# Moving the head of two attentions into the stages before them, in one kernel of four macaron layers

## The chip, the cores and the metric

The kernel runs on one core of a Trainium2 chip. A core has five engines, each with its own instruction queue: TensorE (PE, matmuls; PEld is its weight load), VectorE (DVE), ScalarE (ACT), GpSimd (POOL) and SyncE (SP, DMA issue). An engine takes its queue in order; waits between engines are semaphores. The metric is the device time of one execution in microseconds, as the median of several executions. One more execution is profiled, and all rows of profiles and traces come from it.

## The reference, cut to what matters

The input is eight sequences of 512 tokens of width 128. It runs through a chain of residual blocks, each fed with a layer norm of the running x:

```python
x = x + 0.5 * L0_ffn(ln(x)); x = x + L0_attn(ln(x)); x = x + 0.5 * L0_ffn(ln(x))
x = x + 0.5 * L1_ffn(ln(x)); x = x + L1_attn(ln(x)); x = x + 0.5 * L1_ffn(ln(x))
x = x + 0.5 * L2_ffn(ln(x)); x = x + L2_attn(ln(x)); x = x + 0.5 * L2_ffn(ln(x))
x = x + 0.5 * L3_ffn(ln(x)); x = x + L3_attn(ln(x)); x = x + 0.5 * L3_ffn(ln(x))
```

The change touches these parts:

- `L1_ffn`: sixteen experts of width 64, of which each token takes four (chosen by group and rank), and one shared expert of width 128; `silu(x Wg) * (x Wu)`, weighted, times `Wd`.
- `L1_attn`: sixteen heads of width 8 over the sequence, softmax, with positional encoding before and a norm after. `L3_attn`: the same shape, causal, without encoding and norm.
- `L2_ffn`: a gated feed-forward net whose inputs are rounded in blocks of 16 to a grid of eight values. `L2_attn`: a gated linear recurrence along the tokens. `L3_ffn`: relu net of width 512.

## The kernel before, in words

Everything stays on the chip between the load of x and the store. Tokens lie on partitions in x (`x[b]` is 128 x 4 x 128 for sequence b); the stages transpose to features on partitions. `_STAGES` at the end lists the order: `l0_ffn`, `l0_attn`, `l0_ffn`, `l1_ffn`, `l1_attn`, `experts_layer2`, `l3_attn`, `l3_ffn`. Each stage opens its own pools of SBUF and PSUM and closes them at its end. A scheduler orders the instructions of each engine when the program is built, by dependences, free buffers and the order of emission; `in_order` (L373) ties chosen engines to the order of emission.

**The experts** (`l1_ffn` L836, `experts` L901, `routed` L869). For every sequence there are ten steps. Step e does two matmuls with the weights of two experts (tiles "pg" and "pu"), Silu on ACT (L920), the product with pu on DVE (L921), the product with the token's shares of these experts (tile "big", two PSUM banks, L928), and the down projection of the step before into "po". The last step turns the result back (yT, tile "mm", L938 to L940) and adds it to x (L433). Between the steps `routed(b + 1)` makes the next sequence's norm, transposes and choice of experts; its `ranks` use DVE, and POOL at L957. In PSUM it holds eight banks: po 1, mm 1, pg 2, pu 2, big 2.

**The second use of the experts** is woven with all of layer 2 and the first relu net in `experts_layer2` (L1111): `rounded_ffn` twice, `recurrence` and `relu_ffn` hand in pieces with a slot each, and the list of all pieces, sorted by slot, is emitted in that order. `_EXPERTS`, `_STARTS`, `_STEPS` and the tables `_ROUNDED_FFN`, `_RECURRENCE`, `_RELU_FFN` hold the slots; a slot is a place in the order and no time. There "mm" and "pg" have two buffers, "pu" one.

**The attention** (`attention` L1448). For a sequence, `projections` gives seven pieces: four of the norm (L405 to L413), the transpose xT (L1574), q and k (two matmuls, then "lead", L1541, and "trail", L1543, which together carry the full precision in two rounded halves) and the values v (L1559). `spread_out` (four times, g = 0 to 3) puts four heads at a time onto blocks of 32 partitions (qkT, L1587). `maxima` computes scores once only to take each row's maximum: a matmul of 32 rows into the tile "first" (three buffers), in the causal case a mask added by a second matmul, then a reduction on DVE (L1620). There are 64 such matmul pieces per sequence; the causal case packs short rows together, so that DVE has 44 reductions for them. After every 16 a copy on POOL spreads the maxima (L1626). `maxima_turned` transposes them (L1658 to L1662, tile mT). Then `weighted` computes the scores again, subtracts the maximum by a further matmul with mT, takes the exponential on ACT (L1728) and multiplies with v into "av". In the loop of `weighted(b)`, whose PE order is fixed, the maxima of sequence b + 1 are done two per step, and projections of sequence b + 2 and the end of sequence b - 1 come at the slots of `_SLOTS`.

At the start of each attention nothing of this is there yet for sequence 0:

```python
            for b in range(2):
                for piece in self.projections(b):
                    piece()
                for g in range(4 if b == 0 else 2 if causal else 1):
                    self.spread_out(b, g)
            for _ in range(64 + _SLOTS[key]["lead"]):
                read = next(maxima)()
                if read:
                    read()
            self.maxima_turned(0)
```

So the projections of sequences 0 and 1, the spreads, the 64 maxima of sequence 0 and four of sequence 1 (`lead`) stand ahead of the first weighted score.

Of the kernel before, what the change touches and what calls it, by code (L numbers as in the profile page):

```python
# [26 lines left out]
P = 128  # L27
# [175 lines left out]
def _attention_pack(p, wq, bq, wk, bk, wv, bv, wo, bo):  # L203
# [40 lines left out]
_IN_ORDER = 4.5  # L244
_STARTS = (18, 27, 46, 64)
_STEPS = (8, 8, 8, 6.5)
# [4 lines left out]
    "x_in": -5,  # L251
# [10 lines left out]
    "apply": 1.5,  # L262
    "turned": 2.5,
# [4 lines left out]
    "sums": 7.5,  # L268
    "added": 7.5,
}  # L270
_RELU_FFN = {
    "stats": -1,
    "apply": 0,
    "turned": 2.5,
    "wide": (3.5, 4, 5, 5),
    "product": 6,
    "added": 7.5,
}


class _Kernel:
    def __init__(self, ctx, tc, u, packs, out):
# [3 lines left out]
        const = ctx.enter_context(tc.tile_pool(name="const", bufs=1))  # L286
        self.ln_pool = ctx.enter_context(tc.tile_pool(name="ln", bufs=3))
# [13 lines left out]


# [134 lines left out]
    def l0_ffn(self):  # L437
        nc, tc = self.nc, self.tc
        w = lambda n: self.w["l0f", n]
        with ExitStack() as s:  # L440
            keep = s.enter_context(tc.tile_pool(name="keep", bufs=1))
            sb = s.enter_context(tc.tile_pool(name="sb", bufs=2))
            ps = s.enter_context(tc.tile_pool(name="ps", bufs=2, space=bass.MemoryType.PSUM))
# [36 lines left out]
    def l0_attn(self):  # L480
# [8 lines left out]
        with ExitStack() as s:  # L489
            keep = s.enter_context(tc.tile_pool(name="keep", bufs=1))  # L490
            sb = s.enter_context(tc.tile_pool(name="sb", bufs=2))
            ps = s.enter_context(tc.tile_pool(name="ps", bufs=3, space=bass.MemoryType.PSUM))
# [343 lines left out]
    def l1_ffn(self):  # L836
# [3 lines left out]
        with ExitStack() as s:  # L840
            self.ps = s.enter_context(tc.tile_pool(name="ps", bufs=2, space=bass.MemoryType.PSUM))
            self.rings = {"mm": 1, "pg": 2, "pu": 2}
# [3 lines left out]
            for b in range(NB):  # L846
                ahead = self.routed(b + 1) if b + 1 < NB else iter(())
                experts = self.experts(b)
                for step in range(10):
                    ordered = self.both if (b, step) in self.aside_at else ()  # L850
                    with self.in_order(*ordered):
                        next(experts)
                        next(ahead, None)
                        if (b, step) in self.aside_at:
                            next(self.aside_at[b, step], None)
                for _ in ahead:
                    pass

    def open_experts(self, s):
        nc, tc = self.nc, self.tc  # L860
        keep = s.enter_context(tc.tile_pool(name="keep", bufs=1))
        self.sb = s.enter_context(tc.tile_pool(name="sb", bufs=2))
# [194 lines left out]
    def layer2_constants(self, ctx):  # L1057

        nc = self.nc
        keep = ctx.enter_context(self.tc.tile_pool(name="layer2_keep", bufs=1))  # L1060
# [29 lines left out]
        for name in ("w_gate", "w_up"):  # L1090
# [5 lines left out]
            pt = self.ps.tile([P, NC, P], F32, name="mm", bufs=1)  # L1096
# [8 lines left out]
        pt = self.ps.tile([P, NC, P], F32, name="mm", bufs=1)  # L1105
# [5 lines left out]
    def experts_layer2(self):  # L1111

        tc = self.tc
        with ExitStack() as s:
            self.fsb = s.enter_context(tc.tile_pool(name="fsb", bufs=2))
            self.ps = s.enter_context(tc.tile_pool(name="ps", bufs=2, space=bass.MemoryType.PSUM))
# [11 lines left out]
            def switch():  # L1128
                inner.close()
                self.asb = s.enter_context(tc.tile_pool(name="asb", bufs=2))  # L1130
# [10 lines left out]
            todo.append((_EXPERTS * NB - .001, switch))  # L1141
            todo.sort(key=lambda t: t[0])
# [226 lines left out]
    def l3_ffn(self):  # L1369
# [4 lines left out]
        with ExitStack() as s:  # L1374
            sb = s.enter_context(tc.tile_pool(name="sb", bufs=2))
            ps = s.enter_context(tc.tile_pool(name="ps", bufs=2, space=bass.MemoryType.PSUM))
# [30 lines left out]
    def attention_constants(self, ctx):  # L1407
# [4 lines left out]
        keep = ctx.enter_context(self.tc.tile_pool(name="heads", bufs=1))  # L1412
# [35 lines left out]
    def attention(self, key, causal):  # L1448
# [9 lines left out]
        nc, tc = self.nc, self.tc  # L1458
        with ExitStack() as s:
            keep = s.enter_context(tc.tile_pool(name="keep", bufs=1))  # L1460
            sb = s.enter_context(tc.tile_pool(name="sb", bufs=2))
            ps = s.enter_context(tc.tile_pool(name="ps", bufs=2, space=bass.MemoryType.PSUM))
            self.key, self.causal, self.sb, self.ps = key, causal, sb, ps
            self.bv = keep.tile([P, L], F32, name="bv")
            nc.gpsimd.tensor_copy(
                self.bv.rearrange("p (c d) -> p c d", c=NC), self.wide(self.w[key, "bv"])
            )
            self.seqs = [{} for _ in range(NB)]
            maxima = (m for b in range(NB) for m in self.maxima(b))
            for b in range(2):  # L1470
                for piece in self.projections(b):
                    piece()
                for g in range(4 if b == 0 else 2 if causal else 1):
                    self.spread_out(b, g)
            for _ in range(64 + _SLOTS[key]["lead"]):
                read = next(maxima)()
# [3 lines left out]
            with self.in_order(mybir.EngineType.PE):  # L1480
                for b in range(NB):
                    between = self.between(b)
                    for at, step in enumerate(self.weighted(b)):
                        step([m for m in (next(maxima, None), next(maxima, None)) if m])
# [3 lines left out]
            for piece in self.attended(NB - 1):  # L1488
                piece()

# [21 lines left out]
    def pair(self):  # L1512
        return self.ps.tile([P, 2, L], F32, name="pair")

    def projections(self, b):

        nc, sb, key = self.nc, self.sb, self.key
        w = lambda n: self.w[key, n]
        q = self.seqs[b]
# [3 lines left out]
        def end():  # L1523
            xn = q["xp"]
            norm[3]()
            if key == "l1a":
                q["xp"] = sb.tile([P, NC, D], F32, name="xp", bufs=4)
# [3 lines left out]
        def turned():  # L1531
            q["xT"] = self.turned(q["xp"], "xT")

        def halves():
            p = self.pair()
            q["lead"] = sb.tile([P, 2, L], F32R, name="lead", bufs=1)
# [327 lines left out]
```

## Time and profile before

| what | value |
|---|---|
| median of 3 runs | 2401.47 us (2400.5 to 2409.54) |
| the profiled execution | 2393.91 us |
| its span in the trace | 2392.2 us |
| mean granted clock of PE | 0.928 |
| PE busy | 2111.3 us (88%) |
| DVE busy | 1639.6 us (69%) |
| ACT busy | 1268.1 us (53%) |
| POOL busy | 660.8 us (28%) |
| share of the chain that ended last | PE 56%, DVE 24%, POOL 8%, ACT 7% |

Busy times add up what an engine did over the whole span; matmuls are pipelined and their ends are modelled, so a busy PE is not PE at its peak. The granted clock is the share of full speed that TensorE got. The last instruction of `l1_ffn` that writes x starts at 747.12 us, that of `experts_layer2` at 1859.46 us, by the trace. The costliest group is the reduction of `maxima` (864 of them, 534.8 us on DVE), the second the exponential (512, 436.3 us on ACT); both attentions are in these groups.

### The profile page before, as it was taken

The page shows a single profiled execution, that of the slowest core. Times are in us where ns is not written, and L with a number is a line of the kernel's source. Part 1 is how long each engine was busy: PE and PEld are TensorE (multiplying, and loading weights), DVE is VectorE, ACT ScalarE, POOL GpSimd, SP SyncE. Part 2 cuts the span into 40 slices and gives each one's busy share as a digit, 9 for nine tenths or more (in the row PEclk, how much of TensorE's full clock was granted, in tenths as well). Part 3 has the DMA queues.
Part 4 walks back from the last instruction along what each step waited for, and adds up shares of the span by engine and source line. Part 5 has one row for each costly group of instructions (what it writes and reads, how often), then busy time and mean ns, then how long its engine had stood idle before and what let it go on. Part 6 is the DMA issues. An engine that isn't in the chain of part 4 may idle for free.

```text
span 2392.2 us, 30012 instructions
## 1 busy us (share of the span) xinstructions
PE 2111.3 (88%) x10907; PEld 1011.7 (42%) x10967; DVE 1639.6 (69%) x3830; ACT 1268.1 (53%) x1855; POOL 660.8 (28%) x923
## 2 busy tenths in 40 slices
PE   7679999879998988999987999897778999999989
PEld 3344444434444433333333444355544444444434
DVE  5566775478886888888817889889864556666611
ACT  3546664323332276777762447667674145555554
POOL 1123443023211011111112234456552023333330
PEclk9779998989998599999997999999999779999999
DMA  3000000000000000000000000000000000000001
GB/s 123 1 1 1 1 1 1 14 10 1 1 1 1 0 1 1 1 1 1 1 1 7 1 1 1 1 0 1 1 0 1 0 1 1 1 1 1 1 1 35
DMA packets 10036, 13.08 MB, mean 5 GB/s; under 512 B 416, under 2 KB 8736, under 8 KB 9760
## 3 DMA queue, kind: packets, MB, share of 16 engines
q1 hardware_dynamic: 7776, 10.11, 1.3%
q8 instruction: 86, 1.41, 0.2%
q10 hardware_dynamic: 2112, 1.05, 0.2%
q14 instruction: 62, 0.51, 0.1%
HBM read 9.06 MB, written 2.10 MB: 5 GB/s over the span
## 4 chain that ended last, share of the span: by engine, by line
PE 56%; DVE 24%; POOL 8%; ACT 7%; issue 4%; DMA 0%; ACTq 0%; DVEq 0%; SPq 0%; POOLq 0%
PE pair L314 11%; PE av L314 8%; PE first L314 7%; PE mm L314 7%; PE po L314 5%; DVE max L1620 3%; PE pu L314 3%; ACT e L1728 3%; PE pg L314 3%; PE ck L314 2%; DVE act L921 2%; PE pr L314 2%; POOL ge L957 1%; PE ph L314 1%; DVE act L928 1%
## 5 line engine op out<-in xcount | busy, mean ns | idle before, releaser
L1620 DVE TENSOR_REDUCE max<-first 128x1 f32<-128x512 f32 (+3 forms) x864 | 534.8, 664 | 193.4 <-PE first L314 169.8
L1728 ACT ACTIVATE e<-pair 128x1024 f32<-128x1024 f32 (+3 forms) x512 | 436.3, 864 | 240.6 <-PE pair L314 227.8
L314 PE MATMUL first<-qkT 32*128 32x512 f32 (+3 forms) x1024 | 337.2, 474 | 29.5 <-DVE max L1620 28.1
L314 PE MATMUL pair<-qkT 32*128 32x512 f32 (+3 forms) x1024 | 223.7, 456 | 20.9 <-ACT e L1728 14.6
L314 PE MATMUL av<-e,v 128*32 128x512 f32 (+3 forms) x2048 | 239.7, 537 | 1.0
L314 PEld LDWEIGHTS pair<-qkT 32*128 32x128 f32 x1024 | 95.7, 186 | 233.7 <-ACT e L1728 133.4
L314 PE MATMUL pair<-mT,max_rows 32*128 32x512 f32 (+3 forms) x1024 | 191.5, 375 | 1.8 <-DVE mT L1662 1.8
L314 PEld LDWEIGHTS first<-qkT 32*128 32x128 f32 x1024 | 152.5, 198 | 94.5 <-DVE max L1620 86.2
L920 ACT ACTIVATE act<-pg 128x512 f32<-128x512 f32 x144 | 85.6, 596 | 195.3 <-PE pg L314 130.8
L1730 POOL TENSOR_SCALAR_AFFINE_SELECT e<-e 128x256 f32<-128x256 f32 x256 | 103.4, 407 | 252.4 <-ACT e L1728 252.0
L314 PE MATMUL pu<-xT,w_moe 128*128 128x512 f32 x288 | 154.9, 621 | 11.6 <-DVE act L921 10.9
L314 PE MATMUL po<-act,w_moe 128*128 128x512 f32 x288 | 157.2, 631 | 6.9 <-DVE act L928 4.3
L314 PE MATMUL pg<-xT,w_moe 128*128 128x512 f32 x288 | 152.4, 616 | 2.9 <-ACT h L1213 1.6
L921 DVE TENSOR_TENSOR act<-act,pu 128x512 f32<-128x512 f32 x144 | 97.8, 679 | 32.3 <-PE pu L314 26.8
L1626 POOL COPY copies<-max 128x128 f32<-128x128 f32 x64 | 22.7, 410 | 343.8 <-DVE max L1620 343.8
L314 PEld LDWEIGHTS pair<-mT,max_rows 32*128 32x128 f32 x1024 | 97.2, 189 | 3.6 <-DVE mT L1662 3.3
L928 DVE TENSOR_TENSOR act<-act,big 128x512 f32<-128x512 f32 x128 | 86.4, 678 | 11.6 <-PE big L314 10.5
L1587 ACT CAST qkT<-pair 128x1024 fp32r<-128x1024 f32 x64 | 64.7, 1013 | 42.0 <-PE pair L314 41.5
L314 PEld LDWEIGHTS pu<-xT,w_moe 128*128 128x128 f32 x288 | 51.5, 195 | 75.5 <-issue 37.8
L314 PEld LDWEIGHTS po<-act,w_moe 128*128 128x128 f32 x288 | 48.8, 192 | 63.9 <-issue 26.1
L423 PE MATMUL mm<-w_const,xn 128*128 128x128 f32 x192 | 38.9, 320 | 40.9 <-DVE xn L340 25.0
L314 PEld LDWEIGHTS pg<-xT,w_moe 128*128 128x128 f32 x288 | 52.0, 195 | 54.1 <-issue 42.8
(402 smaller groups left out, 4230.5 us busy)
## 6 DMA issues: line engine op xcount, KB each, us to landing
w_moe<-in_moe SPq DMA_DIRECT2D x1, 2392.0 KB, 14.0
out<-x SPq DMA_DIRECT2D x8, 256.0 KB, 2.3
x<-in_u ACTq DMA_DIRECT2D x4, 256.0 KB, 6.5
x<-in_u SPq DMA_DIRECT2D x4, 256.0 KB, 6.5
w_mixer<-in_l0a SPq DMA_DIRECT2D x1, 960.5 KB, 8.2
w_mixer<-in_l1a SPq DMA_DIRECT2D x1, 769.0 KB, 4.1
w_ffn<-in_l0f SPq DMA_DIRECT2D x1, 578.0 KB, 7.3
w_ffn<-in_l2f SPq DMA_DIRECT2D x1, 560.0 KB, 3.3
```

Of the source, the lines that this page charges most:

```text
L314: self.nc.tensor.matmul(out, lhsT, rhs, start=start, stop=stop)
L423: self.nc.tensor.transpose(pt[:, c, :], xn[:, c, :], self.ident)
L920: nc.scalar.activation(act, pg, AF.Silu)
L921: nc.vector.tensor_tensor(act, act, pu, ALU.mult)
L928: nc.vector.tensor_tensor(act, act, pw[:, e % 2, :], ALU.mult)
L957: nc.gpsimd.tensor_tensor(ge.rearrange(flat), ge.rearrange(flat), self.wide(before, m), ALU.mult)
L1587: self.nc.scalar.copy(t, p)
L1620: nc.vector.tensor_reduce(mx[:, c, j, gs[0] : gs[-1] + 1], sc, AX.X, ALU.max, negate=True)
L1626: nc.gpsimd.tensor_copy(copies[:, :, :, :, g], mx[:, :, :, g].unsqueeze(3).to_broadcast([P, NC, 4, 8]),)
L1728: nc.scalar.activation(e[:, :, :n], sc[:, :, :n], AF.Exp, scale=scale)
L1730: nc.gpsimd.affine_select(e[:, :, :P], e[:, :, :P], pattern=[[0, 2], [1, P]], compare_op=ALU.is_ge, fill=0.0, base=0, channel_multiplier=-1,)
```

## The change

The head of an attention (the value bias bv, seven pieces of `projections(0)`, four of `spread_out(0, g)`, 64 of `maxima(0)`) becomes a generator of 75 pieces, `attention_head`, that begins before the stage in front of it has ended. In `l1_ffn` it begins at step 31 of 80 (b = 3, step 1) and goes on every 0.6 of a step; in `experts_layer2` it begins at slot 84 and goes on every 0.55 of a slot. While it runs there it borrows that stage's PSUM: "pair" becomes the experts' "big" (one buffer), "first" becomes "mm" (two buffers). For that, `l1_ffn` gives one bank of "pu" to "mm". The tiles that outlive the stage lie in a pool "early" on the other side of SBUF. All pools are made with `reuse_waits="tile"`. `seqs` becomes `turns` in the attention, since both stages now hold their own state at once. Slots of layer 2 change, and `_IN_ORDER` with them.

```diff
-_IN_ORDER = 4.5
-_STARTS = (18, 27, 46, 64)
-_STEPS = (8, 8, 8, 6.5)
+_IN_ORDER = 3
+_STARTS = (18, 27, 46, 68)
+_STEPS = (8, 8, 8, 6)
...
 _ROUNDED_FFN = {
-    "x_in": -5,
+    "x_in": -4,
...
 _RECURRENCE = {
-    "apply": 1.5,
-    "turned": 2.5,
+    "apply": 2.5,
+    "turned": 3,
...
-    "sums": 7.5,
-    "added": 7.5,
+    "sums": 8,
+    "added": 8,
...
 _RELU_FFN = {
-    "stats": -1,
-    "apply": 0,
-    "turned": 2.5,
-    "wide": (3.5, 4, 5, 5),
-    "product": 6,
-    "added": 7.5,
+    "stats": -2,
+    "apply": 2,
+    "turned": 4.5,
+    "wide": (5.5, 6, 7, 7),
+    "product": 8,
+    "added": 11.5,
...
+_HEADS = {"l1a": (31, 0.6), "l3a": (84, 0.55)}
+
+def _heads_at(key, step):
+    first, each = _HEADS[key]
+    return sum(step <= first + k * each < step + 1 for k in range(75))
...
+    def pool(self, name, bufs, **kw):
+        return self.tc.tile_pool(name=name, bufs=bufs, reuse_waits="tile", **kw)
...
     def l1_ffn(self):
-            self.rings = {"mm": 1, "pg": 2, "pu": 2}
+            self.rings = {"mm": 2, "pg": 2, "pu": 1}
...
                 for step in range(10):
+                    at = 10 * b + step
+                    if at == _HEADS["l1a"][0]:
+                        self.begin_attention("l1a", False)
+                    heads = _heads_at("l1a", at)
                     ordered = self.both if (b, step) in self.aside_at else ()
                     with self.in_order(*ordered):
...
+                    for _ in range(heads):
+                        next(self.head)
...
     def experts_layer2(self):
+            first, each = _HEADS["l3a"]
+            todo.append((first - .001, partial(self.begin_attention, "l3a", True)))
+            todo.extend((first + k * each, lambda: next(self.head)) for k in range(75))
             todo.sort(key=lambda t: t[0])
...
     def attention(self, key, causal):
         with ExitStack() as s:
+            s.push(self.begun.pop_all())
+            self.sb = s.enter_context(self.pool("sb", 2))
+            self.ps = s.enter_context(self.pool("ps", 2, space=bass.MemoryType.PSUM))
+            self.banks = {"pair": ("pair", 2), "first": ("first", 3)}
+            for _ in self.head:
+                pass
+            for piece in self.projections(1):
+                piece()
+            for g in range(2 if causal else 1):
+                self.spread_out(1, g)
+            for _ in range(_SLOTS[key]["lead"]):
+                read = next(self.all_maxima)()
...
+    def begin_attention(self, key, causal):
+        self.key, self.causal = key, causal
+        self.begun = ExitStack()
+        self.early = self.begun.enter_context(self.pool("early", 1, side="right"))
+        self.banks = {"pair": ("big", 1), "first": ("mm", 2)}
+        self.turns = [{} for _ in range(NB)]
+        self.all_maxima = (m for b in range(NB) for m in self.maxima(b))
+        self.head = self.attention_head()
+
+    def attention_head(self):
+        self.bv = self.early.tile([P, L], F32, name="bv")
+        self.nc.gpsimd.tensor_copy(
+            self.bv.rearrange("p (c d) -> p c d", c=NC), self.wide(self.w[self.key, "bv"])
+        )
+        for piece in self.projections(0):
+            piece()
+            yield
+        for g in range(4):
+            self.spread_out(0, g)
+            yield
+        for _ in range(64):
+            read = next(self.all_maxima)()
+            if read:
+                read()
+            yield
```

The tiles xp, xT, lead, trail, max, copies and qkT of even sequences move to "early"; their number of buffers per sequence stays the same.

## The prediction, made before the changed kernel was run

> **What bounds the kernel now.** I read the slices of the page first, to see which engine is full where.
>
> ```profile
> PE   7679999879998988999987999897778999999989
> ...
> DVE  5566775478886888888817889889864556666611
> ...
> PEclk9779998989998599999997999999999779999999
> ```
>
> PE is nearly full almost everywhere. The odd slices of 59.8 us are those with PE at 9 and its clock low: the 14th (5; 777 to 837 us), the 32nd and 33rd (7; from 1854 us). There PE is slow, not loaded. Next I cut both places by stage, with the busy time of each engine in each stretch (length, then PE, PEld, DVE, ACT, POOL, then the granted clock). The first three rows are sequences 3, 4 and 7 of the experts, the fourth the start of the first attention, the fifth the end of layer 2, the sixth the start of the second attention.
>
> ```profile
> 607.40:636.10 28.70, 27.90 (x85) 12.45 (x85) 24.32 (x67) 10.22 (x16) 6.51 (x8) 1.00 0.00 1
> 636.10:665.10 29.00, 28.26 (x85) 12.41 (x85) 23.83 (x67) 10.19 (x16) 6.33 (x8) 1.00 0.00 1
> ...
> 721.60:747.10 25.50, 24.02 (x61) 9.79 (x60) 14.70 (x31) 4.93 (x9) 1.87 (x3) 1.00 0.00 0
> 747.10:812.40 65.30, 55.40 (x130) 28.62 (x130) 56.55 (x115) 10.54 (x13) 9.78 (x14) 0.63 0.00 1
> 1755.00:1860.20 105.20, 82.48 (x291) 45.50 (x289) 53.80 (x155) 56.48 (x103) 38.02 (x38) 0.92 0.00 1
> ...
> 1860.20:1922.40 62.20, 57.81 (x181) 31.18 (x182) 39.03 (x77) 11.04 (x14) 3.72 (x8) 0.66 0.00 0
> ```
>
> The two starts last 65.3 and 62.2 us, with ACT and POOL all but idle and the clock at 0.63 and 0.66. The chain of waits through the first, in order of time:
>
> ```profile
> 745.70 0.67 PE mm L938 x4
> ...
> 774.90 34.27 PE first L314 x57
> 809.17 1.05 PE pair L1658 x4
> ...
> 812.38 2.79 PE pair L314 x5
> ```
>
> More than half of it is sequence 0's first scores, which nothing covers. The timeline says which engine sets their pace: one run of 62 maxima on DVE in the first attention, and PE's weight load waiting for each; in the second attention DVE waits for PE.
>
> ```profile
> 772.97 37.15 DVE L1620 TENSOR_REDUCE max<-first 128x1 f32<-128x512 f32 x62
> 780.28 0.28 PEld L314 LDWEIGHTS first<-qkT 32*128 32x128 f32 x1 [0.32 <-DVE max L1620]
> ...
> 1894.36 0.69 DVE L1620 TENSOR_REDUCE max<-first 128x1 f32<-128x512 f32 x1 [0.25 <-PE first L314]
> ```
>
> 37.15 us / 62 = 0.598 us per maximum in the first (DVE sets it); 0.94 us in the second (1894.36 to 1895.30), where PE does scores and mask at half clock.
>
> **What goes.** The compiled order of both programs has the same instructions on every engine but for two more ACT table loads (1.28 us each; ACT is a third busy in the experts, so nothing). All 64 maxima of sequence 0 in the first attention, and all 44 in the second, now stand on the tile "mm" among the experts' or layer 2's instructions. No DMA moves; SP's queue is unchanged. What is left between the last transposes of the stage before and the first finished weighted score is sequence 1's chain, since PE's order has it ahead: stage transposes 0.66, its own transposes 0.66, xT copy 0.58, q and k 1.98, lead 1.26, trail 1.41, spread 1.17 (772.87 to 774.04), transposed maxima 1.12, m_lead 0.59, mT 0.74, and nine hand-offs near 0.15: 11.5 us, say 12. In the second attention two spreads and three masked scores more, 14 us. So:
> - first attention: 812.38 - 745.70 = 66.7 us becomes 12: -54.7
> - second: 1922.36 - 1858.70 = 63.7 us becomes 14: -49.7
>
> Together -104.4 us, before what the stages in front pay.
>
> **What the experts pay.** An expert matmul costs 0.86 us on PE (starts at 702.67 and 703.53). A sequence has 27 of them (23.2), eight shares at 0.215 (1.7) and transposes and gate (2.2): 27.1 of some 29 us. DVE's busy time per sequence 3 to 7 is 24.3, 23.8, 22.8, 22.7, 14.7 us, in 28.7, 29.0, 27.5, 29.0 and 25.5 us. Added to PE: scores 64 x about 0.24 (15.4), spread 16 x 0.235 (3.8), q, k, v and transposes 3.3. Added to DVE: 64 x 0.598 (38.3), trail and v 2.2. The order puts 3, 16, 17, 17, 11 maxima into sequences 3 to 7, and the projections and spreads into 3. The fuller engine then needs 34.9 (PE), 33.4, 33.0, 32.9 (DVE) and 26.6 (PE): 160.8 us in place of 139.7. Two engines that feed each other are not both full: DVE's best minute of layer 2 is 55.24 of 60, PE's best of the experts 58.77 of 60. Between them, at 0.94, it is 171 us, **+31**. Ends: +15 (PE alone: four sequences of 27.1 and one of 24.0 are 132.4, plus 22.5, against 139.7), +48 (nothing hidden: DVE's 40.5, and 8 for "big"). "big" is a new wait: its one buffer serves the shares and now seven pieces too; a share that waits for a qkT copy (1.01) holds up the expert matmuls behind it in PE's queue, and DVE's product with the share after them.
>
> The new rings go with this. "pu" has one buffer: a matmul into it waits for the product at L921, and the whole PE queue behind it. Two matmuls, 1.7 us, stand between; the product takes 0.68. Layer 2 already has this ring, and its sequence 1 takes 29.6 us (y at 1314.77 and 1344.34) against 28.7 to 30. I take nothing; without the cover it is 0.7 us x 72 = 50 us, but then DVE is far behind and the +48 case holds already. On POOL, xp (1.1 us), bv (0.61) and four copies (0.41) are moved in; a copy waits for the sixteenth maximum, and a rank's "ge" can stand behind it: 0 to 4 x 1.3, in the 0.94.
>
> **What layer 2 pays.** The slots of layer 2 end later (relu 121.5, scores 124.4, not 117); the scores, from slot 84 on, fall on its last 105 us, where DVE is idle for 51, ACT for 49, PE for 22.7 us. Added to PE at full clock: 16 scores of 512 at 0.58 (starts 1873.03, 1873.61), 16 of 384 at 0.54, 8 doubles near 0.65, 4 quadruples near 0.85, so 26.5, and 6.8 for spread and projections: 33 us. 33 - 22.7 = 10.6 at the least by this row; 2.4 less if the last relu product (5.88 us at half clock against 3.44) stays warm, more since the tail is one chain (rounding, relu) and each inserted score delays it. **+15**; ends +6 and +33 (none hidden). Moving the other slots costs between -5 and +10: I take 0, as the stage's load sets its length and not the numbers.
>
> **Clock.** After both starts the weighted steps run at half clock for some 14 us, 4.2 us a pair of steps (818.62 to 822.83) against 2.75 (829.50 on): 4.8 us lost each time. Twelve us of a thin chain may still lower it, as at 750 to 770 (0.71 and 0.78). **-4**, ends 0 and -10.
> "TensorE: Matmul & The Clock Gate", Part 1, says one busy window of about 3.4 us lifts the throttle. This trace has PE over 0.9 busy from 810 to 826 us before it lifts. By the page the sum would be -7 in place of -4.
>
> **Pools tile-wise.** Orders before the experts are unchanged and a few waits lighter, on instructions that PE releases anyway (xT at 423.33). After the first attention xT (1257.17, 8.14 us idle, released by DVE yn) could go 4 us earlier, but DVE's next step stands behind the cast of the shares: **-1**, ends 0 and -2.
>
> **Sum:** -104.4 + 31 + 15 - 4 - 1 = -63 us. Against the profiled execution's own time, 2393.9 (span 2392.2, and 1.7 around it that stay): 2331. The median of the runs is 2401.5, 7.6 above, so **2338**.
>
> **Rivals.**
> - *Almost all hides*: the experts pay 21 (their fuller engine at 1.0), layer 2 pays 6, clock and pools give 10: -87, 2314. For it: the scores are single short instructions between long ones. Against: no stretch of this trace has DVE above 92% for a minute.
> - *DVE becomes the bound and nothing hides*: +48 and +33, 2 for clock and pools: -25, 2376. For it: DVE was at 85% in sequence 3. Against: PE and DVE both have idle time in both stages.
> - *Slower*: each maximum is a closed round trip through the two "mm" banks, with the PE queue stopped behind it: 0.50 + 0.69 and hand-offs, 1.3 us x 64, with mask 1.55 x 44, and 8 for "big": 159 us against 104 and 5 gained, +50, 2451. It decides from about 0.94 us of stage time per maximum, (104 + 5 - 8) / 108. Against: two banks, and matmuls of other tiles between most scores in the order.
> - *The order is not what runs*: the scores still end up behind the stage: no change, 2401. The compiled order speaks against it.
>
> **How the numbers follow.** Forecast 0.57, almost all hides 0.24, nothing hides 0.14, slower 0.04, no change 0.01. The ends of all terms give a gain of 13 to 100 us; leaving out a tenth on each side, 2305 to 2378. A measurement can tell about 0.5%, 12 us, from no change: faster 0.92 (part of "nothing hides" is within 12 us), same 0.04, slower 0.04.
>
> **What would show it.** Right: 64 and 44 maxima read "mm"; the experts' last y at about 777 instead of 746; the first weighted score some 12 us after it; no slice with a clock near 0.5 in mid kernel; DVE above 90% in sequences 4 to 6. Wrong: PE's score waiting for DVE by more than 0.3 us on most maxima; a shares matmul waiting for qkT; layer 2 longer by over 33 us; expert sequences over 40 us.

## The result, and the profile after

The changed kernel takes 2380.43 us (median of 4 runs, 2377.55 to 2383.18); the kernel before takes 2402.27 us beside it. The ratio is 0.9902, 95% interval 0.9882 to 0.9921: 22 us faster, where the forecast said 63 and gave 23 as the smallest gain of its range. The profiled execution takes 2380.11 us (span 2378.4), so between the two profiled executions there are only 13.8 us: the one of before lay 8 us under its median.

The slices of the changed kernel's page (PE busy, DVE busy, granted clock, 59.5 us each):

```profile
PE   7679999879998888999887999897789899999989
...
DVE  5556775468888788888827889988766556666621
...
PEclk9778998979999999999998999998988999999999
```

The two holes in the clock (a 5 in the 14th slice before, 7 7 in the 32nd and 33rd) are gone, as forecast. So the starts did go. What came in their place shows in the busy time by stage (length, then PE, PEld, DVE, ACT, POOL, then the clock). Before, with sequences 3 to 7 of the experts, the start of the first attention (last y to mT), the end of layer 2 (last y to last ryT) and the start of the second attention (last ryT to m_lead):

```profile
607.37:746.39 139.02, 135.10 (x387) 58.56 (x387) 107.61 (x283) 44.42 (x69) 25.18 (x32) 1.00 0.00 1
746.39:811.58 65.19, 55.38 (x128) 28.60 (x128) 56.42 (x114) 9.98 (x13) 9.78 (x14) 0.64 0.00 1
1610.84:1857.96 247.12, 193.33 (x804) 119.25 (x802) 176.99 (x458) 159.54 (x303) 124.53 (x120) 0.92 0.00 1
1857.96:1920.93 62.97, 57.73 (x181) 31.38 (x182) 38.72 (x77) 10.27 (x13) 3.72 (x8) 0.68 0.00 0
```

The same four stretches of the changed kernel:

```profile
609.05:794.57 185.52, 174.58 (x489) 72.13 (x487) 153.37 (x378) 50.34 (x77) 33.46 (x43) 0.98 0.00 1
794.57:806.72 12.15, 7.34 (x32) 4.16 (x32) 8.09 (x22) 3.35 (x5) 1.27 (x2) 1.00 0.00 1
1603.61:1886.60 282.99, 231.69 (x929) 139.86 (x929) 198.61 (x510) 165.11 (x310) 127.83 (x122) 0.89 0.00 1
1886.60:1906.35 19.75, 14.97 (x58) 8.98 (x59) 9.80 (x25) 4.56 (x6) 2.47 (x6) 0.83 0.00 0
```

The starts fall by 53.0 and 43.2 us. The stages in front grow by 46.5 and 35.9. PE's busy time says why: +39.5 us in the experts with 7 us more idle time (3.9 to 10.9), +38.4 in layer 2 with its idle time as it was (53.8 to 51.3). Almost nothing of the moved work found a hole. Not all of the 38.4 us need be the moved work: the clock of this stretch is 0.89 instead of 0.92, of which more below.

All experiments are read by the same stages, each the distance between the starts of two instructions (y is the experts' output, m_lead the rounded maxima ahead of mT, oT the attention's output and ryT the relu net's): E, first to last y of the experts; A, that last y to m_lead of sequence 0; B, the first attention's last oT to the first y of the second use of the experts; Y, first to last y there; R, its last y to the last ryT; C, last ryT to m_lead of the second attention.

| kernel | median us | ratio (95%) | E | A | B | Y | R | C |
|---|---|---|---|---|---|---|---|---|
| before | 2399 to 2402 | 1 | 202.6 | 63.9 | 66.3 | 296.1 | 247.1 | 63.0 |
| changed | 2380.4 | 0.9902 (0.9882 to 0.9921) | 251.1 | 9.1 | 60.5 | 300.5 | 283.0 | 19.8 |
| pools_only | 2390.7 | 0.9958 (0.9944 to 0.9972) | 203.6 | 56.4 | 66.0 | 297.4 | 246.3 | 61.6 |
| slots_only | 2387.1 | 0.9947 (0.9932 to 0.9962) | 203.3 | 57.9 | 63.1 | 300.5 | 246.0 | 62.8 |
| l1a_only | 2387.5 | 0.9953 (0.9938 to 0.9967) | 251.2 | 9.1 | 64.8 | 297.7 | 248.8 | 61.5 |
| l3a_only | 2380.2 | 0.9907 (0.9880 to 0.9934) | 203.2 | 57.8 | 63.1 | 300.5 | 282.8 | 19.8 |
| old_slots | 2386.8 | 0.9941 (0.9921 to 0.9962) | 251.2 | 10.8 | 70.0 | 297.5 | 275.4 | 23.0 |
| cut_dve | 2363.1 | 0.9847 (0.9823 to 0.9871) | 239.9 | 9.8 | 60.4 | 298.4 | 269.7 | 21.4 |
| cut_pe | 2350.2 | 0.9793 (0.9774 to 0.9813) | 234.6 | 11.4 | 61.8 | 299.2 | 273.9 | 17.2 |
| tied2 | 2411.2 | 1.0051 (1.0031 to 1.0070) | 281.1 | 9.9 | 59.8 | 300.7 | 279.1 | 20.5 |
| wide_l1a | 2389.7 | 0.9958 (0.9942 to 0.9973) | 258.3 | 11.0 | 60.4 | 298.4 | 282.1 | 21.8 |
| score128 | 2373.3 | 0.9884 (0.9857 to 0.9910) | 243.3 | 9.8 | 60.3 | 298.7 | 281.8 | 21.9 |
| wide_l3a | 2376.7 | 0.9890 (0.9871 to 0.9909) | 203.6 | 56.4 | 66.0 | 297.5 | 277.8 | 16.5 |
| wide_l3a_new | 2378.9 | 0.9907 (0.9892 to 0.9922) | 203.5 | 56.4 | 61.7 | 298.8 | 274.1 | 20.2 |
| wide_both | 2380.4 | 0.9925 (0.9897 to 0.9953) | 258.2 | 11.0 | 64.7 | 296.9 | 277.6 | 17.8 |
| mix_l3a | 2371.3 | 0.9877 (0.9860 to 0.9894) | 203.6 | 56.3 | 59.8 | 300.7 | 275.9 | 16.4 |
| mix_both | 2375.8 | 0.9896 (0.9877 to 0.9915) | 251.2 | 10.8 | 60.5 | 300.6 | 275.9 | 16.4 |
| mix_l3a_fast | 2368.9 | 0.9865 (0.9849 to 0.9881) | 203.6 | 56.4 | 59.8 | 300.6 | 277.4 | 14.9 |

E repeats to 1 us between kernels with the same code there, so a difference of 5 us in E is the edit's. B and the attentions vary by some us from one profiled execution to the next. The medians come from different rounds, each with its own kernel before beside it (2398.8 to 2402.3), so a difference of 2 or 3 us between two rows is within their intervals.

### The profile page after: what moved, and what is told of

Same layout as the page of the kernel before. It is cut to its first block, busy times and chain, and to the rows that moved or that the text cites. A ratio compares the mean times of both kernels' runs of the same rounds, so it can differ in the third digit from the quotient of the medians.

```text
span 2378.4 us, 29959 instructions
## 1 busy us (share of the span) xinstructions
PE 2096.9 (88%) x10907; PEld 998.6 (42%) x10967; DVE 1630.9 (69%) x3830; ACT 1270.5 (53%) x1857; POOL 662.1 (28%) x923
## 3 DMA queue, kind: packets, MB, share of 16 engines
q10 hardware_dynamic: 2112, 1.05, 0.2%
## 4 chain that ended last, share of the span: by engine, by line
PE 59%; DVE 23%; POOL 7%; ACT 6%; issue 4%; DMA 0%; ACTq 0%; DVEq 0%; SPq 0%; POOLq 0%
PE pair L329 11%; PE mm L329 8%; PE av L329 8%; PE po L329 6%; PE pu L329 5%; PE first L329 4%; DVE max L1671 4%; PE pg L329 3%; ACT e L1779 3%; PE ck L329 2%; DVE act L942 2%; PE pr L329 2%; PE big L329 1%; PE ph L329 1%; DVE xn L355 1%
## 5 line engine op out<-in xcount | busy, mean ns | idle before, releaser
L1671 DVE TENSOR_REDUCE max<-first 128x1 f32<-128x512 f32 (+3 forms) x756 | 468.2, 664 | 183.2 <-PE first L329 156.0
L329 PE MATMUL first<-qkT 32*128 32x512 f32 (+3 forms) x896 | 268.0, 443 | 30.5 <-DVE max L1671 28.9
L329 PEld LDWEIGHTS first<-qkT 32*128 32x128 f32 x896 | 119.9, 185 | 69.2 <-DVE max L1671 67.0
L1671 DVE TENSOR_REDUCE max<-mm 128x1 f32<-128x512 f32 (+3 forms) x108 | 70.9, 665 | 37.6 <-PE mm L329 30.3
L438 PE MATMUL mm<-w_const,xn 128*128 128x128 f32 x192 | 38.4, 320 | 42.3 <-DVE xn L355 26.7
L978 POOL TENSOR_TENSOR ge<-ge,w_moe 128x64 f32<-128x64 f32 (+1 forms) x32 | 42.8, 1338 | 117.5 <-DVE ge L976 111.9
## 6 DMA issues: line engine op xcount, KB each, us to landing
w_moe<-in_moe SPq DMA_DIRECT2D x1, 2392.0 KB, 13.8
```

The source lines that it names most:

```text
L329: self.nc.tensor.matmul(out, lhsT, rhs, start=start, stop=stop)
L438: self.nc.tensor.transpose(pt[:, c, :], xn[:, c, :], self.ident)
L978: nc.gpsimd.tensor_tensor(ge.rearrange(flat), ge.rearrange(flat), self.wide(before, m), ALU.mult)
L1671: nc.vector.tensor_reduce(mx[:, c, j, gs[0] : gs[-1] + 1], sc, AX.X, ALU.max, negate=True)
```

## The experiments

My theory after the first reading: each score costs TensorE about 0.6 us between expert matmuls, not 0.24, and that is why E grew by 48.5 and not by 31. Rivals: VectorE is the bound there; or the rings (the numbers of PSUM buffers: two for "mm", one for "pu") and "big" are.

### The parts one by one

**pools_only**: no early head, old slots and rings, pools tile-wise. The pool "early" on the other side of SBUF stays, with xp and the other tiles in it.

```diff
-                    if at == _HEADS["l1a"][0]:
-                        self.begin_attention("l1a", False)
-                    heads = _heads_at("l1a", at)
+                    heads = 0
...
-            todo.append((first - .001, partial(self.begin_attention, "l3a", True)))
-            todo.extend((first + k * each, lambda: next(self.head)) for k in range(75))
```

and `attention` calls `begin_attention` itself, with the projections and spreads of both sequences ahead of the maxima as before.

> Both attentions begin at their own start, with the slots and rings of before; only the pools are tile-wise. Theory 'pools': the 5.9 us that the changed kernel gains where the second use of the experts begins (xT copy 11.2 us earlier, of which 5.3 were there already) come from the pools: 2402 - 6 = 2396 us, a stage boundary with the xT copy no longer waiting 8 us for yn. Rival, as forecast: pools are worth 1 us (2401), and the 5.9 us come from elsewhere.

It is 9 to 10 us faster (2390.7 against 2399.65 beside it), but not at the place I read it from: B is 66.0. The gain is in A, 63.9 to 56.4. The timeline of before at that place (PE, then POOL):

```profile
745.70 0.66 PE L938 MATMUL mm<-w_const,yT 128*128 128x128 f32 x4 [0.73 <-ACT yT L935]
749.12 0.66 PE L1574 MATMUL pair<-w_const,xp 128*128 128x128 f32 x4 [2.77 <-POOL xp L1529]
750.59 3.61 PE L314 MATMUL pair<-xT,w_mixer 128*128 128x512 f32 x4 [0.81 <-ACT xT L1576]
```

```profile
747.98 2.14 POOL L1529 TENSOR_TENSOR xp<-xn,w_mixer 128x512 f32<-128x512 f32 x2 [9.65 <-DVE x L433]
```

and in pools_only:

```profile
699.63 1.09 POOL L1579 TENSOR_TENSOR xp<-xn,w_mixer 128x512 f32<-128x512 f32 x1 [6.27 <-DVE xn L426]
749.53 0.66 PE L955 MATMUL mm<-w_const,yT 128*128 128x128 f32 x4 [0.73 <-ACT yT L952]
750.97 0.66 PE L1624 MATMUL pair<-w_const,xp 128*128 128x128 f32 x4 [0.78 <-DVE y L957]
752.30 1.98 PE L327 MATMUL pair<-xT,w_mixer 128*128 128x512 f32 x4 [0.68 <-ACT xT L1626]
```

Before, POOL waits 9.65 us for the very last x of the experts, though sequence 0 has been ready for 200 us. In pools_only the first xp starts at 699.63, 48 us earlier, while the experts still run. So the transposes of xp start 1.44 us behind those of yT instead of 3.42, and the matmuls for q and k run in 1.98 us, not 3.61. The first maximum starts 10.9 us behind the last y instead of 18.4. My reading is that before, the whole pool of the stage had to be free; but two things changed at once, the tile-wise release and the place of xp in "early", and no run here tells them apart. "The pools" below means both.

**slots_only** (as above, with the new slots):

> No early head; pools tile-wise and layer 2's new slots alone. The kernel with pools alone takes 2390.7. Forecast's reading: the slots are worth nothing, between -5 and +10: 2391. Theory 'slots delay the relu net': layer 2's end is 10 us later without any score in it, 2400. Third: the new slots, not the head, are what gains in the run with the second head alone: 2380.

3.6 us faster than pools alone by the medians, with intervals that overlap. By the stages the slots gain in B (59.8 to 63.1 in all runs with the new front part, 64.7 to 70.0 in all with the old) and lose some 3 in Y; from pools_only to slots_only that is -2.9 and +3.1, so the stages do not show where the 3.6 us are. The relu net is not delayed by them (R 246.0 against 246.3).

**l1a_only** (old slots, the lines of `todo` left out) and **l3a_only** (new slots, `heads = 0` and the old rings in `l1_ffn`):

> Only the first attention begins early, in the experts (new rings, pools tile-wise); layer 2 has the slots of before and no scores in it. By the stages of the changed kernel's trace: experts +48, start of the attention -53, clock -1, boundary -6: 2402 - 12 = 2390 us, the experts' last y at 794.6 us. Rival: the halves disturb one another and the first head alone gives the forecast's -28 or more: 2374 or less, last y near 777.

> Only the second attention begins early, in layer 2 with the new slots; the experts have the rings and the order of before. By the stages of the changed kernel's trace: boundary -6, layer 2 +36 to +40, start of the attention -43, clock -3, a loss of 6 inside the second attention: 2402 - 10 = 2392 us, between 2386 and 2398. Rival: most of the net gain of 22 us is here, 2382 or less.

The first head alone adds nothing measurable to pools alone: 2387.5 against 2390.7, with intervals that overlap. Its stages: E +47.6, A -47.3. The second head is worth 6.9 us over the slots alone (2387.1 to 2380.2): R +36.8, C -43.0. And l3a_only is as fast as the whole change, which was the rival of its expectation (2392). So, added in this order and by the medians, some 9 to 10 of the 22 us are the pools', 4 the slots', 7 the second head's, and none the first's. Only the pools' part, and slots and second head together (0.9958 to 0.9907), are clear of the intervals.

**old_slots**: the change with the tables of before.

> The changed kernel with the slots of layer 2 as before (sum, steps, relu tables and the in-order bound), both heads early. Theory 'slots': the relu net's new slots set its last product 11 us later than its work needs, and layer 2 pays 15 instead of 36 to 40: 2380 - 20 = 2360 us. Theory 'price': 33 us and more of scores on TensorE are paid wherever the other pieces stand: 2380, plus or minus 6. Third: the old slots put layer 2's relu pieces behind the scores, and it is slower: 2390.

Neither theory in full: R is 7.6 us shorter, C 3.2 longer, and B has the long stretch of the old front part (70.0, the longest of all). "The slots are why layer 2 pays 36" falls: with the old ones it still pays 29.

### What a score costs among the experts

**cut_dve** and **cut_pe**:

```diff
-                    mx[:, c, j, gs[0] : gs[-1] + 1], sc, AX.X, ALU.max, negate=True
+                    mx[:, c, j, gs[0] : gs[-1] + 1], sc[:, :, :64] if b == 0 else sc, ...
```

```diff
+            w = 64 if b == 0 else n
-                sc[:, k, :],
+                sc[:, k, :w],
-                q["kT"][gs[k]][r, :n],
+                q["kT"][gs[k]][r, :w],
...
-                if causal:
+                if causal and b > 0:
```

> The changed kernel; the maxima of sequence 0 in both early heads are taken over the first 64 keys only (the softmax's offset is another number, its quotient the same), so that each reduction on VectorE is some 0.45 us shorter and TensorE's work is unchanged. The stages to read: the experts' first to last y (251.1 us now, 202.6 before) and layer 2's last y to last ryT (283.0 now, 247.1 before). Theory 'VectorE is the bound': the experts fall by 64 x 0.45 x 0.7 = 20 us to 231, layer 2 by 10. Theory 'TensorE's price of a score': neither falls by more than 5 us; total 2375 to 2381.

> As the run with the short reductions, and the scores of sequence 0 in both heads are computed for these 64 keys alone and without the masks, so TensorE too has less to stream. Theory 'TensorE's price of a score' (0.42 us of its own time and 0.19 us on the matmul after it): the 0.42 falls to some 0.1, 64 x 0.32 = 20 us less in the experts, to 231; in layer 2 the scores and masks fall from 33 us to about 10, 20 us less, to 263; total 2340. If the price is not the streaming but the change between 32-row and 128-row matmuls, the experts stay above 240. Theory 'VectorE': no further fall beside the other run.

E falls by 11.2 with the short reductions and by 5.3 more with the short scores. So neither theory holds alone: VectorE has a part in E, and TensorE's streaming is worth a quarter of what I expected of it. The busy times of sequences 3 to 7, first cut_dve, then cut_pe:

```profile
609.38:783.75 174.37, 171.53 (x489) 71.98 (x487) 126.64 (x377) 50.39 (x77) 32.67 (x43) 0.99 0.00 1
```

```profile
606.23:775.37 169.14, 164.50 (x489) 73.80 (x487) 126.83 (x378) 50.40 (x77) 32.70 (x43) 0.97 0.00 1
```

Against the changed kernel, cut_dve takes 8.1 us from PE's idle time (10.9 to 2.8) and 3.0 from its busy time. So the 7 us of idle that the change added go with the length of the reductions. The changed kernel's waits of PE in these sequences (total us, times, longest):

```profile
PE po L329 <- DVE act L949: 2.2, 2, 1.4
PE mm L1128 <- DVE w_downT L1129: 2.1, 1, 2.1
PE pg L329 <- ACT act L941: 1.9, 4, 0.7
PE pu L329 <- DVE act L942: 1.9, 2, 1.5
```

No score waits for "mm", no share for qkT: what waits are mostly the experts' own matmuls, for products that share DVE's queue with reductions of 0.69 us. Of the rings, 2.0 us show in sequence 1 (35.6 instead of 33.5, with no head in it), and the waits for the one buffer of "pu" come to 1.9 us here (last line; none before). No run has the new rings without a head, so their share in sequences 3 to 7 is not measured by itself.

With short scores most of the price is still there: in cut_pe a score of 64 columns takes 0.22 us to the next start, and the pair of expert matmuls behind it 0.96 instead of 0.86.

Layer 2 answers differently. Its end (R), first cut_dve, then cut_pe:

```profile
1591.63:1861.33 269.70, 220.91 (x929) 134.01 (x927) 184.93 (x510) 166.31 (x310) 127.00 (x122) 0.92 0.00 1
1588.83:1862.68 273.85, 222.84 (x889) 138.23 (x888) 184.86 (x510) 165.88 (x311) 126.94 (x122) 0.88 0.00 1
```

cut_dve is 13.3 us shorter than the change, of which 10.8 are PE's busy time for the same matmuls, at a clock of 0.92 instead of 0.89, and 2.5 its idle time. cut_pe has no masks and short scores, and R is 4.2 us longer than that, at 0.88; 263 was expected. So R moves by some 10 us with the clock, and the price of a score in layer 2 can't be read from these two.

**tied2** ties TensorE's order of the experts to the order of emission and emits two scores at a time:

```diff
+                with self.tied():
+                    reads = [next(self.all_maxima)() for _ in range(n)]
+            for read in reads: ...
...
+                        if at >= _HEADS["l1a"][0] and step < 9:
+                            with self.tied():
+                                next(experts)
```

> The changed kernel; in the experts the scores are emitted two at a time, and TensorE's order is tied so that 31 pairs stand back to back on different rows of the array (the changed kernel has 15 pairs and 34 alone). Theory 'price': a lone score costs 0.61 us, a pair 0.62 together: 34 x 0.61 + 15 x 0.62 = 30 becomes 31 x 0.62 + 2 x 0.61 = 20.5, 9.5 us less: experts 241.5 us, total 2371. Rival: the ties cost what they bring, or the stall is elsewhere (one buffer of pu, big): 251, total 2380 or more.

A clear miss: 31 us slower than the change. The pairs are there, and two scores take 0.43 us together as they should, but the fixed order waits. Busy time of sequences 3 to 7, and PE's waits in them:

```profile
609.39:824.71 215.32, 187.63 (x491) 78.22 (x491) 158.01 (x376) 51.33 (x78) 32.77 (x43) 0.90 0.00 0
```

```profile
PE mm L937 <- POOL halves L931: 8.2, 2, 4.3
PE mm L329 <- DVE max L1701: 6.2, 5, 3.1
```

PE is idle for 27.7 us instead of 10.9, the granted clock is 0.90 instead of 0.98, and PE's busy time is 13 us longer for the same matmuls. It says nothing against the price; since the ties also fix the experts' own matmuls, it says that the order by readiness was worth more than the pairs.

**wide_l1a**: `"l1a": (12, 0.88)` in place of `(31, 0.6)`.

> The changed kernel; the first attention's head begins at step 12 instead of 31 and takes every 0.88 of a step instead of 0.6, so that 11 maxima instead of 17 fall into one sequence of experts. Theory 'own price and waits for VectorE': TensorE's own 30 us of the head stay, the 11 us of waits that went with the short reductions mostly go: first to last y 243 instead of 251.1, total 2372. Rival 'price alone, each lone score slows the matmul after it': 52 lone scores instead of 34, 251 or more, total 2380 to 2386.

The rival is right: E is 7.2 us longer (its total, 2389.7, lies above the rival's 2386 as well). PE waits less for DVE's products (4.5 us instead of 6.2 in all of E), but 52 scores stand alone instead of 34.

**score128** asks for the price itself:

```diff
+            whole = b == 0 and not causal
-                q["qT"][gs[k]][r, bass.ts(c, P)],
-                q["kT"][gs[k]][r, :n],
+                self.zero if whole else q["qT"][gs[k]][r, bass.ts(c, P)],
+                q["kT"][gs[k]][:, :n] if whole else q["kT"][gs[k]][r, :n],
```

> The changed kernel; in the experts each score of sequence 0 has all 128 rows of the array instead of 32, with a left side of zeros, and the maxima of this sequence are a constant (the softmax has a fixed offset there). TensorE streams as many columns as before and VectorE reduces as much; only the change of form between a 32-row score and the 128-row matmuls around it is gone, and with it what two scores side by side save. Theory 'the change of form costs 0.19 us on the matmul after it': 49 places x 0.19 = 9 less, 15 pairs x 0.25 = 4 more, experts first to last y 246 against 251.1. Theory 'only its own streaming and VectorE's waits': 251 to 255.

E falls by 7.8 us, although two scores side by side now share nothing. The chain of the changed kernel in sequence 4 (a score, then a pair of expert matmuls behind it; start, time to the next link):

```profile
651.58 0.44 PE mm L438 x4
652.02 0.43 PE mm L329
652.45 1.05 PE pg L329 x2
653.50 0.43 PE mm L329
653.93 1.05 PE pu L329 x2
```

and the timeline of score128:

```profile
662.57 0.27 PE L1119 MATMUL mm<-w_const,w_r 128*128 128x128 f32 x1
662.60 0.48 PE L329 MATMUL mm<-qkT,zero 128*128 128x512 f32 x1
662.91 1.02 PE L329 MATMUL pg<-xT,w_moe 128*128 128x512 f32 x2
663.77 1.02 PE L329 MATMUL pu<-xT,w_moe 128*128 128x512 f32 x2
```

There the pair takes 0.86 us (662.91 to 663.77). In the trace of before the same addition stands around the shares, which have 32 rows too:

```profile
642.74 1.02 PE L314 MATMUL po<-act,w_moe 128*128 128x512 f32 x2
643.69 0.50 PE L314 MATMUL big<-shareT,shares 32*128 32x512 f32 x2
644.12 1.12 PE L314 MATMUL po<-act,w_moe 128*128 128x512 f32 x2
645.08 1.02 PE L314 MATMUL pg<-xT,w_moe 128*128 128x512 f32 x2
645.94 1.02 PE L314 MATMUL pu<-xT,w_moe 128*128 128x512 f32 x2
```

The pair in front of the shares takes 0.95 us, the one behind 0.96, a pair with no 32-row neighbour 0.86. In the changed kernel's trace it is one matmul each: 0.52 us to the next start in front of a score and 0.53 behind it, where an expert matmul otherwise takes 0.43. (The 1.05 of the chain above is a pair with 32-row matmuls on both sides.) So I take what scores add where expert matmuls stand on both sides: from the start of the matmul in front to the start of the second one behind, less twice 0.43; medians over sequences 3 to 7, with the number of places:

| | one score adds | two side by side add |
|---|---|---|
| 32 rows (changed) | 0.62 (14) | 0.63 (11) |
| 32 rows, 64 columns (cut_pe) | 0.42 (15) | 0.42 (10) |
| 128 rows (score128) | 0.24 (14) | 0.47 (11) |

So a place with one score or two costs 0.62 us: 0.42 from the score to the next start, 0.10 in the matmul behind it and 0.09 in the one in front. This is shown: with the form equal a lone score costs 0.24, and these 25 places alone make up 7.1 of the 7.8 us. It fits wide_l1a too, which has 58 places instead of 49 (5.6 of its 7.2 us).

The Trainium skill has both halves. "TensorE: Matmul & The Clock Gate", section "Why this matters for your kernels", says that a single matmul of 32 rows takes as long as one of 128 and that the gain lies in several side by side. This trace agrees with the second (two for 0.63) and not with the first (0.62 against 0.24 between the experts). "TensorEngine Tiling (Array Packing)", section "Key Properties", says that a change of tiling mode drains the engine; it gives no price, and here the matmuls on the two sides of the change take 0.09 and 0.10 us more.

### Layer 2, and a better version

**wide_l3a** has only the second head, the old slots, and `"l3a": (72, 0.6)`; **wide_l3a_new** the new slots and `(80, 0.6)`; **wide_both** is the old slots, `(12, 0.88)` and `(72, 0.6)`.

> Only the second head, with the old slots of layer 2, in which the relu net ends at slot 117; the head takes slots 72 to 117 instead of 84 to 125. The run with the second head alone and the new slots takes 2380.2. Theory 'nothing of a score is hidden in layer 2': layer 2 pays its 36 us wherever the head lies, last y to m_lead of the second attention 302 us, total 2380. Rival 'the place counts': scores among the fuller first half of the tail leave the relu chain alone, 292 us, total 2372.

> As the run with the second head alone and the new slots, but the head takes slots 80 to 125 instead of 84 to 125. By 'nothing is hidden': 2380, last y to m_lead 302.6 us as there. By 'the place counts': 5 us less, 2375.

> The earlier, thinner first head and the second head with the old slots from 72 to 117 together. If the parts add up as they have so far, this is the time of the second alone plus what the first adds to it (the earlier first head against none): between 2362, if both save 8 to 10, and 2382, if neither does.

R and C together are 294.3 us in both single ones, where the change has 302.8 and pools alone 307.9. By the stages the place counts, with less than the rival gave it (292 was its figure): 8 us, but 3.5 and 1.3 by the medians, which is inside their intervals, so it is not shown. In wide_both the first head takes the gain away again (+3.7 by the medians).

**mix_l3a** takes the new slots but the old relu table with `(72, 0.6)`, **mix_both** adds the first head, **mix_l3a_fast** has `(73, 0.54)`:

```diff
-_STARTS = (18, 27, 46, 68)
-_STEPS = (8, 8, 8, 6)
+_STARTS = (18, 27, 46, 64)
+_STEPS = (8, 8, 8, 6.5)
...
-_HEADS = {"l1a": (31, 0.6), "l3a": (84, 0.55)}
+_HEADS = {"l1a": (31, 0.6), "l3a": (73, 0.54)}
```

> A version meant to be better: only the second head, at slots 72 to 117; the relu net's slots are the old ones, all other slots of layer 2 the new ones (the stage boundary before it took 61.7 to 63.1 us with the new ones, 64.8 to 70.0 with the old, first to last y 298.8 to 300.5 against 296.9 to 297.7). By the sum of stages: 2376.7 - 4 + 2 = 2374 us. Rival, the parts do not add up: 2380.

> As the version meant to be better, and the first attention's head as in the changed kernel besides. Theory 'the first head pays in the experts what it saves at the start' (48.5 against 48.7 by the stages): the same time as without it, 2374, within 4 us. Rival: the first head is worth the 3 us that its single run showed against pools alone (2390.7 to 2387.5): 2371.

> As the version meant to be better, with the second head at 0.54 of a slot from 73 on, which ends at 113 and not at 117. If the scores cost their own TensorE time wherever they lie, no difference: 2374. If the last relu product is what they delay, 2 to 4 us less.

mix_l3a_fast is the fastest version with the whole computation: 0.9865 against 0.9902 for the change, without the first head. Of mix_l3a it is 2.4 us ahead by the medians, within the intervals, and R and C together are 292.3 us in both. mix_both is 4.5 us slower than mix_l3a. Over three comparisons of with and without, the first head costs -3.2, +0.3 and +4.5 us: it brings nothing. What layer 2 does with the second head, first slots_only without it, then mix_l3a_fast (last y to last ryT):

```profile
1606.43:1852.47 246.04, 192.32 (x804) 120.11 (x803) 171.99 (x458) 157.88 (x301) 126.91 (x120) 0.90 0.00 1
```

```profile
1603.70:1881.14 277.44, 231.28 (x942) 140.60 (x943) 206.58 (x514) 164.12 (x309) 131.18 (x126) 0.90 0.00 1
```

PE's busy time grows by 39 us, its idle time falls from 53.7 to 46.2. Even in the fastest version, PE's idle time here takes up 7.5 us of 39.

## Why the prediction was wrong, point by point

- **What goes** was nearly right: forecast 104.4, measured 54.8 (A) and 43.2 (C), 98.0. Between the forecast's own end points (the stage's last transposes to the first matmul with mT) 13.7 us are left where 12 was said (793.87 to 807.52; four reductions of sequence 1, 2.5 us, stand between m_lead and mT on DVE) and 19.0 where 14 was said (1888.81 to 1907.78): the clock is 0.83 there and the last masked scores stand in it.
- **What the experts pay** failed: forecast +31, measured +48.5, and the step is "a score costs PE 0.24 us". I took it from a row where scores stand two by two on different rows of the array; among experts they stand alone in 34 places of 49, and a place costs 0.62 with one score or two. From one start to the next, PE gave the scores 20.7 us where I had 15.4, and the projections and spreads 9.2 where I had 7.1. PE's busy time grew by 39.5, which leaves 9.6 for the slower matmuls beside (49 places at 0.19); 7.0 more idle, and 2.0 in sequences 1 and 2, which I had at nothing for the new rings.
- In the same part, "the fuller engine, divided by 0.94" was the wrong form of sum. PE was at 97% before (135.1 of 139.0), so what is added to it is added to the time; and DVE, at 81 to 88% in sequences 4 to 6 and not over 90, still adds waits. The two do not overlap, they add up.
- **What layer 2 pays** failed by more: forecast +15, measured +35.9 in R, beyond the end of +33. The failed step is "33 - 22.7 = 10.6": PE's own time was sized nearly right (19.6 for scores, 5.5 for masks, 10.8 for projections and spreads, 35.9 in all between starts), but I counted PE's idle time as room. It is for the most part the waiting of a chain (rounding, products, relu), and the chain waits as long with the scores in it: 53.8 us idle before, 51.3 after. PE's longest waits in R of the changed kernel name it:

```profile
PE mm L1253 <- POOL h_r L1070: 14.8, 9, 4.5
PE pu L329 <- DVE h L1238: 9.4, 10, 1.9
PE mm L1253 <- ACT hT L1254: 6.3, 6, 2.5
```

  How much of the 35.9 is a lower clock stays open: the forecast priced PE at full clock, the stretch ran at 0.89, and cut_dve at 0.92 took 10.8 us less of PE for the same matmuls. "Other slots: 0" is by slots_only against pools_only -2.9 in B and +3.1 in Y, so it held by the stages.
- **Clock, -4**: the first attention from m_lead to its last oT took 0.9 us longer, not less, the second 3.1 longer. The first sequence of the second attention did gain 2.7, but pools_only and slots_only, without a head, gain 2.4 and 2.5 there as well; and two later ones lost 2.9 each at a clock of 0.94, which also happens in kernels without any head.
- **Pools, -1** was wrong by itself: alone, with "early", they are worth 9 to 10 us. The forecast weighed two waits (xT at 423.33 and at 1257.17) and not the one at the start of the first attention, where POOL waited 9.65 us. In the change most of it is in the same 65 us that the head takes away, so it is not to be counted twice.
- **The 7.6 us** to the median were of that one execution: the changed kernel's profiled time is its median.
- **What would show it**: right on the 64 and 44 maxima on "mm" and the clock; on the first weighted score too (12.95 us behind the last y); wrong on the last y (794.6, not 777) and on DVE over 90%. Of the signs of error two came: layer 2 beyond 33, and one sequence of 42.2 us. A score waiting for DVE and a share waiting for qkT did not come. So the rival "nothing hides" (+48, +33; 2376) was nearly the truth, but its +48 was luck: it was made of 40.5 of VectorE and 8 for "big", and the runs show some 30 us of TensorE for the scores, 9 for projections and spreads, and up to 11 that go with the length of the reductions; "big" did not show.

## What to carry to other kernels

Before moving work from a bare start into a full stage, compare what one piece costs in the start with what it costs there: here 64 maxima took 38 us at VectorE's pace in the start, and among the experts 30 us of TensorE (0.62 for each place with one score or two), 9 for projections and spreads, and 7 of waits, which left no gain whatever the start looked like. Idle time of an engine inside a chain of dependences need not be room (2.5 us of 38 in the change, 7.5 of 39 in the fastest version); only a run shows whether it takes anything up. And test the small parts of a change alone: here the pools brought nearly half of the gain.

## What was not expected of the hardware

A 32-row score between 128-row expert matmuls adds 0.62 us, two side by side 0.63, of which 0.19 are in the matmuls in front and behind; the same score with 128 rows adds 0.24. In tied2, where TensorE idles for 13% of a stretch, the mean clock is 0.90 instead of 0.98. And the second attention, whose sequences take 51.5 us, has one to three sequences of 54.4 in most runs, at a lower clock; the changed kernel, one of each:

```profile
2009.80:2061.40 51.60, 48.81 (x430) 24.20 (x438) 33.22 (x66) 29.80 (x44) 16.57 (x39) 1.00 0.01 1
2061.40:2115.80 54.40, 51.75 (x430) 25.08 (x436) 33.08 (x66) 29.70 (x43) 16.58 (x39) 0.94 0.00 1
```

The same instructions, 2.9 us more of PE. The 0.94 is a stretch of some 7 us at 0.50 (2091 to 2098 us), and PE is busy without a gap in it and in the 2 us before it. What lowers the clock in these stays open, and so does why the new slots shorten B. How much of layer 2's 35.9 us is the clock stays open too: for the same 929 matmuls in R PE is busy for 231.7 us at 0.89 in the change and for 220.9 at 0.92 in cut_dve.
